# One VectorE product instead of two, moved between two scans, in a selective-scan network

## The chip, the cores and the metric

The kernel runs on one core of a Trainium2 chip. The metric is the device time of one execution in microseconds (us), less being better. The core has five engines that run their own instruction streams and meet at semaphores: TensorE (PE) multiplies matrices into PSUM, VectorE (DVE) and ScalarE (ACT) work on PSUM and SBUF, GpSimd (POOL) on SBUF, and SyncE (SP) issues the DMAs. Each stream runs in its written order: an instruction that waits holds up all behind it on its engine.

## The reference

Four images of 56 x 56 tokens with 96 channels go through two state-space blocks and two blocks of linear attention with a quantised feed-forward part. Nearly all the time is in the selective scans. Cut to that:

```
# for each of 2 layers, 4 images, 4 directions; L = 3136 tokens, 192 channels d, 16 states s
dt  = softplus(W_dt @ dt_raw + bias)            # [d, t]
h_t = exp(dt_t * A[d, s]) * h_{t-1} + dt_t * u_t * B_t[s]
y_t = sum over s of h_t[d, s] * C_t[s]           # summed over directions, plus u * D
# around it: layer norm and projection in; gate, projection, norm, GELU feed-forward out (layer 0);
# a depthwise 3x3 convolution with SiLU ahead of the scan, fusion and layer norm after it (layer 1)
```

## The kernel before, in words

**Rounds.** A scan of 3136 tokens is cut into 7 chunks of 448 tokens. A chunk is 8 rounds: two halves `e` of the channels (96 each) times four groups `q` of states. A round holds 96 channels x 4 states as three tiles of 128 partitions (`g` = 0, 1, 2) by 448 tokens. In all there are 2 x 4 x 4 x 7 x 8 = 1792 rounds.

**What a round does.** `products(n)` makes `du * B` on VectorE for g = 0 and 1, two instructions of 128x448 (L695), with B spread over the partitions in PSUM by one matmul (`spread_b`, L597, one PSUM buffer `b`). The product for g = 2 is made on GpSimd in `begin` (L690), from a copy of B in SBUF. Three scans on VectorE (L702) turn products and decays into states `h`. A decay is `exp(dt * A)` on ScalarE (`decay`, L654), into one PSUM buffer per g. After each scan of round n, ScalarE makes the same decay of round n + 1. Behind the third scan it also keeps the last column (`kept`, L672), and copies the carry into the tile of round n + 2 (`carried`, L667). GpSimd multiplies all three tiles by C in one instruction (`hc`, L744), and TensorE sums over the states (`add_up`, L775), two rounds later. Tiles `h` and `hc` have three buffers each.

**B and C.** `fetch` copies B and C from DRAM to all partitions of a tile `cb`, four DMAs per tile (L533). A tile is used in two rounds of the chunk, `q` and `q + 4`. `prepare(ch, o)` does the steps of a chunk by the number `o` of the round relative to its first: at -9 the rows of B and C go to DRAM, at -5 to -3 step sizes are parked in DRAM and spread over partitions (`dt`, `du`), and at -3 to 0 `fetch` is called. `prepare_on_scalar` and `on_tensor` do the ScalarE and TensorE steps of the same plan (L568 and L489, L590 and L479).

**Side work.** The other stages (norms, projections, GELU, convolutions, attention, feed-forward) run as generators, called lanes here. The loop hands control to them twice per round: at `yield "F"`, ahead of the round's scalar steps, and at `yield "C"`, between scans 0 and 1. Steps marked F are mostly ScalarE work, steps marked C mostly TensorE and VectorE work. A planner with declared costs (`spend`, `room`, `SPARE`, `ACT_LIMIT`, `PE_LIMIT`) limits how much enters a round. A GELU or SiLU step changes ScalarE's tables and changes them back (`exp_and_ln`, L806). `keep_busy` gives TensorE filler matmuls on zeros (L762) in rounds with little of its work. A convolution reads its rows through a window tile `win` (L930).

**Order.** The streams of TensorE, ScalarE, VectorE and GpSimd are in the order in which the code emits them. SP's order is the scheduler's. The lines that fix the order around the change:

```
            products(n)                 # top of round n
            ...                         # prepare, lane steps F, prepare_on_scalar, filler
            begin(n + 1)                # spread_b and GpSimd's product of round n + 1
            ...                         # add_up(n - 2), on_tensor
            for g in range(NG):
                if g == 1:
                    yield "C", n, r
                ...
                scan(n, g)
                ...
                decay(n + 1, g)
            carried(n + 2)
```

Of the kernel before, what the change touches and what calls it, by code (L numbers as in the profile page):

```python
# [11 lines left out]
F32 = mybir.dt.float32  # L12
# [4 lines left out]
ALU = mybir.AluOpType  # L17
# [10 lines left out]
NQ = 4  # L28
# [4 lines left out]
CS = 448  # L33
# [3 lines left out]
NCS = L // CS  # L37
RANK = (12, 6)
NW, LATE_NW = 13, 20
NWIN = 3  # L40
OWN = ()
OWN_TAIL = ()

SPARE = (0.9, 2.4)
ACT_LIMIT, PE_LIMIT = 4.0, 7.0
# [121 lines left out]
class Net:  # L167
    def __init__(self, ctx, tc, aps, at, out):
# [5 lines left out]
        self.dram = pool("dram", bufs=1, space=bass.MemoryType.DRAM)  # L174
        self.nw, self.nwin, self.depth, self.banks, self.ring = NW, NWIN, DEPTH, BANKS, None
        self.setup()
# [350 lines left out]

    def fetch(self, ch, q):

        t = self.sp.tile([128, 2, CS], F32, name="cb", bufs=5)  # L530
        rows = ch.cd.rearrange("(k n) t -> n k t", k=2)
        for s in range(4):
            self.nc.sync.dma_start(t[32 * s : 32 * s + 32], rows[q + 4 * s].partition_broadcast(32))  # L533
        ch.cb.append(t)

    def prepare(self, ch, o):

        nc = self.nc  # L540
        if o == -14:
            self.parameters(ch)
        elif o == -12:
            self.inputs(ch)
        elif o == -9:
            ch.cd = self.dram.tile([2 * NS, CS], F32, tag="cd", name="cd", bufs=3)
            nc.sync.dma_start(ch.cd, ch.cf[: 2 * NS])
        elif o == -5:
            self.times_u(ch)
            ch.dtd = self.park(ch.dtc)  # L550
        elif o == -4:
            ch.dud = self.park(ch.duc)
            self.spread_dt(ch, 0)
        elif o == -3:
            self.spread_du(ch, 0)
        elif o == 0:
            self.spread_du(ch, 1)
            self.spread_dt(ch, 1)
        if -3 <= o <= 0:
            self.fetch(ch, o + 3)  # L560

    def prepare_on_scalar(self, ch, o):

# [30 lines left out]
    def spread_b(self, ch, q):  # L594

        ps = self.psum.tile([128, 512], F32, tag="b", name="b", bufs=1)[:, :CS]
        self.nc.tensor.matmul(ps, self.sel[:, q], self.upper(ch.cf), start=True, stop=True)  # L597
        return ps
# [5 lines left out]
    def scans(self):  # L604

        nc, sp = self.nc, self.sp
        chunks = []
        for l in range(2):
            for i in range(NB):
                for n, (orient, rev) in enumerate(ORDER[l]):
                    for step in range(NCS):
                        ch = Step()
                        ch.l, ch.i, ch.orient, ch.rev, ch.step = l, i, orient, rev, step
                        ch.k = 2 * orient + rev if l == 0 else orient + 2 * rev  # L620
                        ch.c = NCS - 1 - step if rev else step
                        ch.n, ch.first = n, n == 0 and step == 0
                        ch.skip = n == 0
                        ch.last = n == 3 and step == NCS - 1
                        ch.cb, ch.dt, ch.du = [], [], []
                        chunks.append(ch)
        rounds = [(ch, e, q) for ch in chunks for e in range(NE) for q in range(NQ)]
        per = NE * NQ


        da = [self.psum.tile([128, 512], F32, name=f"da{g}")[:, : CS + 4] for g in range(NG)]
        for t in da:
            nc.vector.memset(t, 0.0)

        def steps(n):

            return [(ch, n - per * j) for j, ch in enumerate(chunks[max(0, n // per) : n // per + 3], max(0, n // per))]

        def ahead(n):
            for ch, o in steps(n):  # L640
                self.on_tensor(ch, o)

        for n in range(-14, 0):
            for ch, o in steps(n):
                self.prepare(ch, o)
            for ch, o in steps(n):
                self.prepare_on_scalar(ch, o)
            ahead(n)

        def decay(n, g):  # L650

            if n < len(rounds):
                ch, e, q = rounds[n]
                nc.scalar.activation(da[g][:, INNER], ch.dt[e][:, g], AF.Exp, scale=ch.par.na[:, e, q, g : g + 1])  # L654

        def column(t, at):

            return t[:, at : at + 2 * ROW + 1 : ROW]

        def carried(n):  # L660

            if n < len(rounds):
                ch, e, q = rounds[n]
                hs[n] = sp.tile([128, WIDE], F32, name="h", bufs=3)
                if not ch.step:
                    return
                nc.scalar.copy(column(hs[n], ROW if ch.rev else 1), ch.par.carry[:, e, q])  # L667

        def kept(n):
            ch, e, q = rounds[n]  # L670
            if ch.step < NCS - 1:
                nc.scalar.copy(ch.par.carry[:, e, q], column(hs[n], 2 if ch.rev else CS + 1))  # L672

        def own(n):
            ch, e, q = rounds[n]
            return NQ * e + q in (OWN_TAIL if ch.l and ch.i else OWN)

        hs, bs = {}, {}

        def tokens(t):  # L680

            return self.groups(t, 2)[:, :, :CS]

        def begin(n):

            if n < len(rounds):
                ch, e, q = rounds[n]
                bs[n] = self.spread_b(ch, q)
                if not own(n):
                    nc.gpsimd.tensor_tensor(tokens(hs[n])[:, 2], ch.du[e][:, 2], ch.cb[q][:, 1], ALU.mult)  # L690

        def products(n):
            ch, e, q = rounds[n]
            for g in range(3 if own(n) else 2):
                nc.vector.tensor_tensor(tokens(hs[n])[:, g], ch.du[e][:, g], bs[n], ALU.mult)  # L695

        def scan(n, g):
            ch, e, q = rounds[n]
            c = 1 if ch.step else 0
            way = slice(CS + 1 + c, 1, -1) if ch.rev else slice(2 - c, CS + 2)  # L700
            h = hs[n][:, g * ROW :]
            nc.vector.tensor_tensor_scan(h[:, way], da[g][:, way], h[:, way], 0.0, ALU.mult, ALU.add)  # L702

        carried(0)
        carried(1)
        begin(0)
        self.exp_and_ln()
        self.tables = True
        for g in range(NG):
            decay(0, g)  # L710
        late = []
        for n, (ch, e, q) in enumerate(rounds):
            r = NQ * e + q
            products(n)
            for c, o in steps(n):
                self.prepare(c, o)
            self.half_round()
            strided = [1.5 + 1.5 * ch.orient] * (r % NQ == 2)
            strided += [1.5 + 1.5 * c.orient for c, o in steps(n) for _ in self.projected(c, o)]
            self.spend((0.6, 0.7, 1.7, 0, 0, 0, 0.7, 0.6)[r], (1.3, 1.3, 0, 0, 0, 0, 0.4, 0.4)[r] + sum(strided))  # L720
            yield "F", n, r
            for c, o in steps(n):
                self.prepare_on_scalar(c, o)
            ended = late.pop(0) if len(late) == 2 else None
            if ended:
                self.keep_busy(ended[2])
            begin(n + 1)
            if ended:
                self.add_up(*ended)
            ahead(n)  # L730
            self.half_round()
# [3 lines that stand above are left out]
                if g == 2 and ended and ended[2] == NQ - 1:  # L735
                    self.spend(0.6, 0)
                    self.keep_sums(*ended[:3])
                scan(n, g)
                if g == 2:
                    kept(n)  # L740
                decay(n + 1, g)
            carried(n + 2)
            hc = sp.tile([128, NG, CS], F32, name="hc", bufs=3)
            nc.gpsimd.tensor_tensor(  # L744
                hc, tokens(hs[n]), ch.cb[q][:, 0].unsqueeze(1).to_broadcast([128, NG, CS]), ALU.mult,
            )
            late.append((ch, e, q, hc))
            del hs[n], bs[n]
        for ended in late:
            self.add_up(*ended)  # L750
        self.keep_sums(ch, e, q)
        yield "C", len(rounds), 0
# [619 lines left out]
```

## Time and profile before

| what | value |
|---|---|
| median of 3 runs | 8361.93 us (8339.22 to 8369.98) |
| the profiled execution, its own time | 8364.46 us |
| its span from first to last instruction | 8362.7 us |
| first and last scan | 112.8 and 7983.9 us |
| mean granted TensorE clock | 0.898 of full |
| one scan, mean duration (L702) | 1071 ns, 5376 of them |
| one product with B, mean duration (L695) | 604 ns, 3584 of them |
| one decay, mean duration (L654) | 632 ns, 5376 of them |
| one `hc` (L744) and one GpSimd product (L690) | 2726 and 979 ns, 1792 of each |

In rows of groups, the columns after the count are the busy time in us, the mean duration in ns of one instruction, and the idle time of the engine just before them with what ended it. Instructions overlap at their ends, so a start-to-start distance is a little shorter than a duration. In rows of waits, the columns are the total in us, the number of times, and the longest. In a timeline, a row has its start, its length, the engine, the line, what is written and read, how many instructions are merged, and in brackets the idle time ahead. About 380 us after the last scan are side work of the last image, which the change does not touch.

### The profile page before, as it was taken

Reading aid. Unit: us, or ns where it says so; the run is one execution under the profiler, and the core shown is the slowest. Engines: PE = TensorE matmul, PEld = TensorE weight load, DVE = VectorE, ACT = ScalarE, POOL = GpSimd, SP = SyncE. Lnnn points to the kernel's source line nnn. Section 1 sums busy time; section 2 is a strip of 40 time slices with the busy share of each in tenths; the row PEclk is TensorE's granted clock in tenths of the full one; section 3 lists DMA queues with packets and bytes.
Section 4 is the critical chain, followed back from the end, with each engine's and each line's share of the span. In section 5 each row is a group of like instructions: output and inputs, shape, how many; then the busy total and the mean of one; then the engine's idle time right before and its main releaser. Section 6 shows DMA issues by size and latency. Waiting matters only on the chain. (4 is left out here: it accounts for less than half of the span.)

```text
span 8362.7 us, 119228 instructions
## 1 busy us (share of the span) xinstructions
PE 7469.6 (89%) x33633; PEld 2721.6 (33%) x33633; DVE 7516.6 (90%) x9555; ACT 6109.8 (73%) x12807; POOL 7177.3 (86%) x3991
## 2 busy tenths in 40 slices
PE   7889888898889988898899979988899888998997
PEld 3333233232333223232322323333333333333344
DVE  5999999999998999999998999999999999999921
ACT  5778878776787768786777766777776777767736
POOL 4999989989998999899898998998888888889820
PEclk8899989899999989998898989988899888999986
DMA  5777777678766777677776777676766667666721
GB/s 154 179 188 189 203 179 182 167 175 199 178 174 170 172 188 181 172 177 184 177 175 167 174 185 176 166 170 172 186 166 162 166 173 182 167 160 167 175 57 48
DMA packets 944159, 1417.77 MB, mean 170 GB/s; under 512 B 169410, under 2 KB 936644, under 8 KB 942628
## 3 DMA queue, kind: packets, MB, share of 16 engines
q1 hardware_dynamic: 942720, 1408.34, 68.2%
q8 instruction: 264, 4.33, 0.2%
q14 instruction: 403, 3.30, 0.1%
q10 hardware_dynamic: 772, 1.80, 0.1%
HBM read 1141.42 MB, written 268.14 MB: 169 GB/s over the span
## 5 line engine op out<-in xcount | busy, mean ns | idle before, releaser
L702 DVE TENSOR_TENSOR_SCAN h<-da,h 128x449 f32<-128x449 f32 (+1 forms) x5376 | 5507.1, 1071 | 134.9 <-ACT da L654 79.3
L744 POOL TENSOR_TENSOR hc<-h,cb 128x1344 f32<-128x1344 f32 x1792 | 4884.8, 2726 | 598.8 <-DVE h L702 413.6
L654 ACT ACTIVATE da<-dt,na 128x448 f32<-128x448 f32 x5376 | 3353.1, 632 | 1143.2 <-DVE h L702 1104.4
L695 DVE TENSOR_TENSOR h<-du,b 128x448 f32<-128x448 f32 x3584 | 2019.6, 604 | 182.7 <-PE b L597 112.6
L775 PE MATMUL y<-hc,four 128*32 128x448 f32 x14336 | 1913.0, 609 | 17.8 <-POOL hc L744 17.4
L690 POOL TENSOR_TENSOR h<-du,cb 128x448 f32<-128x448 f32 x1792 | 1754.1, 979 | 141.4 <-DMA cb<-cd 110.1
L762 PE MATMUL y<-w,zeros 128*96 128x448 bf16 x4843 | 1354.0, 397 | 0.0
L597 PE MATMUL b<-cf,sel 128*128 128x448 bf16 x1792 | 680.2, 380 | 631.2 <-DVE h L695 626.6
L762 PEld LDWEIGHTS <-zeros 128*96 128x96 bf16 x4843 | 603.2, 135 | 1111.0 <-issue 965.1
L775 PEld LDWEIGHTS y<-hc,four 128*32 128x32 f32 x14336 | 294.2, 113 | 1182.5 <-issue 660.5
L433 PE MATMUL pp<-U,wd 96*128 96x448 f32 x896 | 664.5, 830 | 12.1 <-DMA U<-u 8.3
L771 PE MATMUL y<-Y,ident 96*96 96x448 f32 x672 | 542.9, 898 | 18.6 <-ACT Y L782 14.3
L919 PE MATMUL ps<-win,dg 64*64 64x220 f32 (+11 forms) x1998 | 547.3, 471 | 0.0
L479 PE MATMUL pp<-cf,wd 12*96 12x448 f32 (+1 forms) x896 | 476.2, 613 | 71.7 <-ACT dtc L489 47.6
L672 ACT COPY carry<-h 128x3 f32<-128x3 f32 x1536 | 301.9, 197 | 282.3 <-DVE h L702 276.2
L504 POOL TENSOR_TENSOR duc<-dtc,U 96x896 f32<-96x896 f32 x224 | 483.1, 2157 | 3.3 <-ACT dtc L491 3.3
L782 ACT COPY Y<-y 96x448 f32<-96x448 f32 x448 | 341.7, 763 | 77.7 <-PE y L775 76.8
L919 PEld LDWEIGHTS ps<-win,dg 64*64 64x64 f32 (+2 forms) x1998 | 239.7, 162 | 321.5 <-issue 289.0
L667 ACT COPY h<-carry 128x3 f32<-128x3 f32 x1536 | 280.2, 182 | 66.3 <-POOL hc L744 63.5
L489 ACT ACTIVATE dtc<-pp,wd 96x448 f32<-96x448 f32 x448 | 281.7, 629 | 31.3 <-PE pp L479 27.4
L597 PEld LDWEIGHTS <-sel 128*128 128x128 bf16 x1792 | 183.8, 103 | 336.1 <-issue 272.7
L827 PEld LDWEIGHTS ps<-avg,w 96*112 96x112 f32 (+2 forms) x1944 | 249.9, 193 | 108.1 <-issue 59.0
(427 smaller groups left out, 5933.9 us busy)
## 6 DMA issues: line engine op xcount, KB each, us to landing
cb<-cd SPq DMA_DIRECT2D x3584, 112.0 KB, 3.9
dt<-dd SPq DMA_DIRECT2D x1792, 168.0 KB, 4.3
du<-dd SPq DMA_DIRECT2D x1792, 168.0 KB, 4.1
dd<-dtc SPq DMA_DIRECT2D x224, 336.0 KB, 3.0
dd<-duc SPq DMA_DIRECT2D x224, 336.0 KB, 3.1
U<-u SPq DMA_DIRECT2D x112, 168.0 KB, 4.7
z<-w SPq DMA_DIRECT2D x56, 224.0 KB, 4.5
u<-w SPq DMA_DIRECT2D x56, 224.0 KB, 3.9
```

Source lines behind the costliest of these rows:

```text
L433: self.nc.tensor.matmul(ch.ps.rearrange("p (a b) -> p a b", b=HS), ch.par.wx[:, e], self.in_order(self.U[e], ch.orient, ch.c * CS, CS), st ...
L504: self.nc.gpsimd.tensor_tensor(in_rows(ch.duc), in_rows(ch.dtc), u[:, :, lo : lo + CS // HS], ALU.mult)
L597: self.nc.tensor.matmul(ps, self.sel[:, q], self.upper(ch.cf), start=True, stop=True)
L654: nc.scalar.activation(da[g][:, INNER], ch.dt[e][:, g], AF.Exp, scale=ch.par.na[:, e, q, g : g + 1])
L690: nc.gpsimd.tensor_tensor(tokens(hs[n])[:, 2], ch.du[e][:, 2], ch.cb[q][:, 1], ALU.mult)
L695: nc.vector.tensor_tensor(tokens(hs[n])[:, g], ch.du[e][:, g], bs[n], ALU.mult)
L702: nc.vector.tensor_tensor_scan(h[:, way], da[g][:, way], h[:, way], 0.0, ALU.mult, ALU.add)
L744: nc.gpsimd.tensor_tensor(hc, tokens(hs[n]), ch.cb[q][:, 0].unsqueeze(1).to_broadcast([128, NG, CS]), ALU.mult,)
L762: self.nc.tensor.matmul(self.y[:C], self.zeros, self.some, start=False, stop=False)
L771: nc.tensor.matmul(o, w, self.in_order(a, ch.orient, ch.c * CS, CS), start=True, stop=False)
L775: nc.tensor.matmul(self.y[32 * n : 32 * n + 32], self.four, hc[:, g], start=n == 3, stop=n == 3 or q == NQ - 1,)
L919: self.nc.tensor.matmul(o[:, a - r0 : e - r0, x0:x1], diag[:, tap], win[:, a + dy - lo : e + dy - lo, x0 + dx : x1 + dx], start=n == 0, st ...
```

## The change

The two products with B of a round become one instruction over 128 x 2 x 448, and it stands ahead of the third scan of the round before. The matmul that spreads B leaves `begin` and is emitted at the end of the round two before. `fetch` is called at -6 to -3 with seven `cb` buffers instead of five. There are four window tiles instead of three. An option to do the third product on VectorE, empty before, is taken out.

```diff
-NWIN = 3
-OWN = ()
-OWN_TAIL = ()
+NWIN = 4
 ...
-        t = self.sp.tile([128, 2, CS], F32, name="cb", bufs=5)
+        t = self.sp.tile([128, 2, CS], F32, name="cb", bufs=7)
 ...
-        if -3 <= o <= 0:
-            self.fetch(ch, o + 3)
+        if -6 <= o <= -3:
+            self.fetch(ch, o + 6)
 ...
         # begin(n)
-                bs[n] = self.spread_b(ch, q)
-                if not own(n):
-                    nc.gpsimd.tensor_tensor(tokens(hs[n])[:, 2], ch.du[e][:, 2], ch.cb[q][:, 1], ALU.mult)
+                nc.gpsimd.tensor_tensor(tokens(hs[n])[:, 2], ch.du[e][:, 2], ch.cb[q][:, 1], ALU.mult)
+
+        def spread_b(n):
+            if n < len(rounds):
+                bs[n] = self.spread_b(rounds[n][0], rounds[n][2])

         def products(n):
-            ch, e, q = rounds[n]
-            for g in range(3 if own(n) else 2):
-                nc.vector.tensor_tensor(tokens(hs[n])[:, g], ch.du[e][:, g], bs[n], ALU.mult)
+            if n < len(rounds):
+                ch, e, q = rounds[n]
+                b = bs.pop(n).unsqueeze(1).to_broadcast([128, 2, CS])
+                nc.vector.tensor_tensor(tokens(hs[n])[:, :2], ch.du[e][:, :2], b, ALU.mult)
 ...
+        spread_b(0)                     # ahead of the loop
         begin(0)
 ...
+        products(0)
+        spread_b(1)
 ...
-            products(n)                 # top of round n
 ...
+                if g == 2:
+                    products(n + 1)     # in the loop over g, ahead of scan(n, 2)
                 scan(n, g)
 ...
+            spread_b(n + 2)             # end of round n
```

More of the change, by code (lines that the diff above doesn't have):

```diff
@@ L672, in kept @@
                 nc.scalar.copy(ch.par.carry[:, e, q], column(hs[n], 2 if ch.rev else CS + 1))
-        def own(n):
-            ch, e, q = rounds[n]
-            return NQ * e + q in (OWN_TAIL if ch.l and ch.i else OWN)
         hs, bs = {}, {}
@@ L687, in begin @@
                 ch, e, q = rounds[n]
-                bs[n] = self.spread_b(ch, q)
-                if not own(n):
-                    nc.gpsimd.tensor_tensor(tokens(hs[n])[:, 2], ch.du[e][:, 2], ch.cb[q][:, 1], ALU.mult)
+                nc.gpsimd.tensor_tensor(tokens(hs[n])[:, 2], ch.du[e][:, 2], ch.cb[q][:, 1], ALU.mult)
+        def spread_b(n):
+            if n < len(rounds):
+                bs[n] = self.spread_b(rounds[n][0], rounds[n][2])
         def products(n):
-            ch, e, q = rounds[n]
-            for g in range(3 if own(n) else 2):
-                nc.vector.tensor_tensor(tokens(hs[n])[:, g], ch.du[e][:, g], bs[n], ALU.mult)
+            if n < len(rounds):
+                ch, e, q = rounds[n]
+                b = bs.pop(n).unsqueeze(1).to_broadcast([128, 2, CS])
+                nc.vector.tensor_tensor(tokens(hs[n])[:, :2], ch.du[e][:, :2], b, ALU.mult)
         def scan(n, g):
@@ L747, in scans @@
             late.append((ch, e, q, hc))
-            del hs[n], bs[n]
+            del hs[n]
+            spread_b(n + 2)
         for ended in late:
```

## The prediction

> **What bounds the kernel now.** I read the engines' shares first, then the costliest groups, then who waited for whom on VectorE, then the timeline.
>
> ```profile
> PE 7469.6 (89%) x33633; PEld 2721.6 (33%) x33633; DVE 7516.6 (90%) x9555; ACT 6109.8 (73%) x12807; POOL 7177.3 (86%) x3991
> ...
> L702 DVE TENSOR_TENSOR_SCAN h<-da,h 128x449 f32<-128x449 f32 (+1 forms) x5376 | 5507.1, 1071 | 134.9 <-ACT da L654 79.3
> ...
> L695 DVE TENSOR_TENSOR h<-du,b 128x448 f32<-128x448 f32 x3584 | 2019.6, 604 | 182.7 <-PE b L597 112.6
> ...
> L690 POOL TENSOR_TENSOR h<-du,cb 128x448 f32<-128x448 f32 x1792 | 1754.1, 979 | 141.4 <-DMA cb<-cd 110.1
> ```
>
> Four engines are busy, but 5507.1 + 2019.6 us of VectorE is the round loop itself. It runs from 112.8 to 7983.9 us: 7871 us for 1792 rounds, 4.39 each. The median distance from one round's first scan to the next is 4.01 us, the bare sum of a round's five VectorE instructions: in most rounds VectorE never waits. Its gaps in the loop sum to only about 440 us. The waits:
>
> ```profile
> DVE h L695 <- PE b L597: 112.6, 143, 4.6
> DVE w L856 <- PE ps L842: 87.8, 21, 12.3
> DVE h L702 <- ACT da L654: 79.3, 165, 2.1
> DVE h L702 <- POOL h L690: 53.2, 26, 10.1
> ```
>
> (Columns: total us, times, longest; the second reaches into the stretch after the loop.) The third decides my forecast. The timeline shows where it comes from: a round in which ScalarE changes its tables.
>
> ```profile
> 2106.98 0.63 ACT L654 ACTIVATE da<-dt,na 128x448 f32<-128x448 f32 x1
> 2107.55 0.18 ACT L667 COPY h<-carry 128x3 f32<-128x3 f32 x1
> 2107.75 1.28 ACT L1038 ACT_TABLE_LOAD   x1
> 2109.04 1.16 ACT L1038 ACTIVATE w<-ps,b 128x448 f32<-128x448 f32 x2
> 2110.22 1.28 ACT L806 ACT_TABLE_LOAD   x1
> 2111.52 1.19 ACT L654 ACTIVATE da<-dt,na 128x448 f32<-128x448 f32 x2
> ```
>
> VectorE in the same stretch:
>
> ```profile
> 2106.77 1.12 DVE L695 TENSOR_TENSOR h<-du,b 128x448 f32<-128x448 f32 x2
> 2107.81 3.05 DVE L702 TENSOR_TENSOR_SCAN h<-da,h 128x449 f32<-128x449 f32 x3
> 2110.78 1.12 DVE L695 TENSOR_TENSOR h<-du,b 128x448 f32<-128x448 f32 x2
> 2112.19 1.09 DVE L702 TENSOR_TENSOR_SCAN h<-da,h 128x449 f32<-128x449 f32 x1 [0.29 <-ACT da L654]
> ```
>
> The last scan of a round ends, ScalarE makes decay 2 (L654), copies a carry, and then does side work until 2111.52; only then comes decay 0, for which the scan at 2112.19 waits. Meanwhile VectorE runs a pair of products, three scans and another pair, about 5.07 us. The burst needs 5.36, so VectorE waits 0.29.
>
> [...] a pair starts 1.04 us before the next scan (2106.77 to 2107.81)[...] after the load at 2107.75 the next instruction starts at once[...]
>
> **The change, part by part.**
>
> *One product for two: -96 us.* [...] No trace shows a 128x2x448 product[...].
>
> *The product moved ahead of the last scan: +197 us.* It leaves the gap between a round's scan 2 and the next round's scan 0. From one scan 2 to the scan 0 two rounds on, VectorE used to have two pairs and three scans, 5.07 us; now one product and three scans, 2.97 + 0.99 = 3.96. ScalarE's order is unchanged: kept, decay 2, carry, side work, decay 0. Relative to the scans, decay 2 can start one product later, while decay 0 is due at the same scan. In the burst shown the wait becomes 5.36 - 3.96 = 1.40 instead of 0.29. Going through all rounds, ScalarE's work from decay 2 to the following decay 0 exceeds 3.15 us in 231 of them (the pairs of Silu or Gelu with two table loads, and the two-fold quantised relu at L1204 to L1206). In 168 of these the scan started within 0.25 us of its decay, in 214 within 1.05. Summing 1.05 less the slack, where positive, gives 197 us. As a cross-check, the same count at the old threshold of 4.2 us gives 75 us of waiting, and the trace has 79.3. The other two decays keep their slack: each still has three scans and a product between its release and its use.
>
> *B's matmul moved from behind the filler matmuls to the end of the round two before: -40.* It is single-buffered, so it still starts after the preceding product and has three scans until it is due. But 49 of the 143 waits, 50 us, come after three or more fillers (L762, 0.28 us each) queued ahead of it. Now it goes first. Queued behind it, when it waits for VectorE, are those fillers, add_up and the next TensorE steps; they may start a product and a scan sooner than now.
>
> *That earlier start is used up by others: +40.* TensorE's steps L590 and L479 wait for ScalarE's copies of the same round, which move one product later; B is due a scan and a product earlier relative to them, in four of eight rounds. GpSimd's hc is also nearer: it is done 2.87 us after scan 2 in the median round, and TensorE will ask for it about then. Bounds 0 and +100; I take the middle.
>
> *B and C six rounds ahead, and the fourth window: -50.* The queue shows the stop that both remove:
>
> ```profile
> 2545.82 1.73 SPq L514 DMA_DIRECT2D du<-dd  x4
> 2560.92 0.47 SPq L930 DMA_DIRECT2D win<-m  x1
> 2561.48 0.53 SPq L514 DMA_DIRECT2D dt<-dd  x1
> ```
>
> A window waits for its buffer for 13.3 us (2547.6 to 2560.9); behind it wait dt and cb; GpSimd waits 12.7 for cb and VectorE 9.6 for GpSimd. Three such stops make 30 of the 53.2 us. I take 45 of these, and 5 of the 34.4 of VectorE's waits for du, of which 15.6 belong to the very first round. Moved earlier in SP's queue are four DMAs per B/C pair; q = 3 will wait for the hc of the round just ended, but du for the same round is issued in front of it and the next in three rounds, so I cost that wait at nothing. If lanes stop the queue elsewhere, du becomes the late one.
>
> *Relief of other waits in the rounds that now stall: -50.* TensorE and GpSimd catch up while VectorE waits 197 us more. The loop's waits on lane results (ps 96, ScalarE's w 38) and the rest of the B waits (about 63) are 197 us; I let a quarter go. Bounds 0 and -150.
>
> Sum: -96 + 197 - 40 + 40 - 50 - 50 = +1 us. The profiled execution took 8364.46 us (span 8362.7), 2.5 above the median of 8361.93: forecast 8365 us.
>
> **The rivals.**
>
> *Slower: ScalarE sets the pace of burst rounds, and nothing is relieved.* The mechanism is decay 0 behind a table change; it decides from 3.15 us of work on. For it: the count reproduces today's 79.3. Without relief and without B's -40, with +40 from TensorE: -96 + 197 + 40 - 50 = +91, about 8455; with the upper TensorE bound 8515.
>
> *Faster: TensorE's earlier start is worth more than its anchors cost.* For it: TensorE waits 626.6 us for the products (B's buffer) and leaves VectorE waiting for ps, w and da. If bursts fall in rounds that other engines delay anyway, half of their cost remains: -96 + 98 - 90 - 50 = -138, about 8225. Against it: slack in the burst rounds is near zero, so nothing else delays them.
>
> *The merged product is no cheaper* (two dimensions handled as two passes): the -96 goes, and with the rest about 8460. [...]
>
> **How the numbers follow.** About 0.5%, 42 us, is what a measurement of this kernel can tell from no change. The even trade 0.40, its own range 8310 to 8425 (30 of these 40 points within 0.5%, 5 on each side); slower, with the unmerged case, 0.33; faster 0.27. So faster 0.32, same 0.30, slower 0.38. The range takes in both main rivals: 8215 to 8490.
>
> **What would show it.** In the profile after: 1792 products of about 1.05 us with a start-to-start near 0.99; scan waits on da up from 79 to about 275 us, nearly all on the first scan of a round; cb and the window's waits gone; waits for b below 113. If the da waits stay under 120 the central step is wrong and the kernel is faster; if b waits double, TensorE's anchors were underrated.

## The result, and the profile after

The changed kernel takes **8580.16 us** (median of 4 runs, 8555.56 to 8585.28), against 8353.1 for the kernel before beside it: 1.0265 times as long, 95% interval 1.0236 to 1.0294. The forecast was 8365 us, with a range up to 8490; the kernel is slower than either. TensorE's mean granted clock was 0.900 in the profiled execution and 0.898 before, so the clock does not explain the loss. Lines of code have moved a little: the scan (L702) is now L701, the decay (L654) L652, the product (L695) L694, B's matmul (L597) L595.

The engines' shares and the costliest groups of the page after:

```profile
PE 7460.7 (87%) x33633; PEld 2730.5 (32%) x33633; DVE 7414.1 (86%) x7763; ACT 6081.2 (71%) x12807; POOL 7182.9 (84%) x3991
...
L701 DVE TENSOR_TENSOR_SCAN h<-da,h 128x449 f32<-128x449 f32 (+1 forms) x5376 | 5522.1, 1071 | 270.6 <-ACT da L652 262.4
...
L694 DVE TENSOR_TENSOR h<-du,b 128x896 f32<-128x896 f32 x1792 | 1904.1, 1063 | 328.5 <-PE b L595 178.2
...
L682 POOL TENSOR_TENSOR h<-du,cb 128x448 f32<-128x448 f32 x1792 | 1757.8, 981 | 46.9 <-DMA cb<-cd 27.1
```

VectorE does 102.5 us less work and is idle longer. Some of its waits (total us, times, longest; the last two also count waits outside the loop):

```profile
DVE h L701 <- ACT da L652: 262.4, 225, 1.9
DVE h L694 <- PE b L595: 178.2, 156, 5.4
DVE w L860 <- PE ps L846: 107.3, 32, 14.5
DVE h L694 <- DMA du<-dd: 51.8, 10, 22.6
```

Sorted over the stretch from the first scan to the last, in us:

| VectorE in the loop | before | after | difference |
|---|---|---|---|
| busy | 7442.9 | 7340.4 | -102.5 |
| waits of a scan for its decay | 79.3 | 262.4 | +183.1 |
| waits of a product for B | 112.6 | 178.2 | +65.6 |
| waits for lane results of TensorE and ScalarE | 124.1 | 161.1 | +37.0 |
| waits of a scan for GpSimd's product | 53.2 | 7.0 | -46.2 |
| other waits, nearly all ahead of a product | 52.6 | 124.9 | +72.3 |
| length of the loop | 7871.0 | 8078.8 | +207.7 |

(Gaps under 0.15 us are left out of the waits.)

The other waits hide more waits for B. The profile names as the releaser what it infers from semaphores, and some products that it puts down to something else, or to nothing ("issue"), start right behind B's matmul. TensorE, then VectorE:

```profile
817.66 0.36 PE L595 MATMUL b<-cf,sel 128*128 128x448 bf16 x1
818.11 1.09 DVE L694 TENSOR_TENSOR h<-du,b 128x896 f32<-128x896 f32 x1 [0.94 <-issue]
```

In the profile after, all but one of the 156 products put down to B start 0.09 to 0.11 us after its matmul ended. So do 69 products among the other waits, with 74.1 us. Before, products put down to B start 0.04 or 0.11 us after it, and 35 of the others 0.09 to 0.11 us, with 26.8 us. Counted with these, B's waits went from 139.4 to 252.3 us, +112.9. The rest went from 25.8 to 50.8, +25.0; most of it is put down to DMAs (18.8 before, 46.2 after).

The first scan starts 9.8 us later, at 122.7 us, and the part behind the last one is 2 us shorter.

The burst that the prediction showed is the same step of the same round here. ScalarE, then VectorE:

```profile
2178.63 0.63 ACT L652 ACTIVATE da<-dt,na 128x448 f32<-128x448 f32 x1
2179.20 0.18 ACT L665 COPY h<-carry 128x3 f32<-128x3 f32 x1
2179.39 1.28 ACT L1042 ACT_TABLE_LOAD   x1
2180.69 1.16 ACT L1042 ACTIVATE w<-ps,b 128x448 f32<-128x448 f32 x2
2181.87 1.28 ACT L810 ACT_TABLE_LOAD   x1
2183.16 1.20 ACT L652 ACTIVATE da<-dt,na 128x448 f32<-128x448 f32 x2
```

```profile
2176.43 1.06 DVE L694 TENSOR_TENSOR h<-du,b 128x896 f32<-128x896 f32 x1
2177.41 3.05 DVE L701 TENSOR_TENSOR_SCAN h<-da,h 128x449 f32<-128x449 f32 x3
2180.38 1.06 DVE L694 TENSOR_TENSOR h<-du,b 128x896 f32<-128x896 f32 x1
2181.36 1.08 DVE L701 TENSOR_TENSOR_SCAN h<-da,h 128x449 f32<-128x449 f32 x1
2183.83 1.09 DVE L701 TENSOR_TENSOR_SCAN h<-da,h 128x449 f32<-128x449 f32 x1 [1.39 <-ACT da L652]
```

The merged row of three scans spans a round boundary: scan 2 of one round, then scans 0 and 1 of the next. Then come the product, scan 2, and the scan 0 that waits. From the end of the first of them VectorE has one product where it had two. The burst is as long as before, and the wait is 1.39 us instead of 0.29; 1.40 was predicted for it.

### The profile page after: what moved, and what is told of

The parts are those of the page before. It is cut to its first block, busy times and chain, and to the rows that moved or that the text cites. A ratio compares the mean times of both kernels' runs of the same rounds, so it can differ in the third digit from the quotient of the medians.

```text
span 8578.1 us, 114910 instructions
## 1 busy us (share of the span) xinstructions
PE 7460.7 (87%) x33633; PEld 2730.5 (32%) x33633; DVE 7414.1 (86%) x7763; ACT 6081.2 (71%) x12807; POOL 7182.9 (84%) x3991
## 5 line engine op out<-in xcount | busy, mean ns | idle before, releaser
L701 DVE TENSOR_TENSOR_SCAN h<-da,h 128x449 f32<-128x449 f32 (+1 forms) x5376 | 5522.1, 1071 | 270.6 <-ACT da L652 262.4
L747 POOL TENSOR_TENSOR hc<-h,cb 128x1344 f32<-128x1344 f32 x1792 | 4885.0, 2726 | 896.4 <-DVE h L701 692.1
L652 ACT ACTIVATE da<-dt,na 128x448 f32<-128x448 f32 x5376 | 3325.3, 630 | 602.2 <-DVE h L701 567.7
L694 DVE TENSOR_TENSOR h<-du,b 128x896 f32<-128x896 f32 x1792 | 1904.1, 1063 | 328.5 <-PE b L595 178.2
L766 PE MATMUL y<-w,zeros 128*96 128x448 bf16 x4843 | 1295.0, 384 | 0.0
L595 PE MATMUL b<-cf,sel 128*128 128x448 bf16 x1792 | 692.7, 387 | 436.5 <-DVE h L694 433.2
L766 PEld LDWEIGHTS <-zeros 128*96 128x96 bf16 x4843 | 638.4, 132 | 1105.2 <-issue 893.0
L477 PE MATMUL pp<-cf,wd 12*96 12x448 f32 (+1 forms) x896 | 478.4, 615 | 185.1 <-ACT dtc L487 104.4
L595 PEld LDWEIGHTS <-sel 128*128 128x128 bf16 x1792 | 191.3, 107 | 659.8 <-issue 655.8
L665 ACT COPY h<-carry 128x3 f32<-128x3 f32 x1536 | 278.4, 181 | 43.4 <-POOL hc L747 41.2
L477 PEld LDWEIGHTS pp<-cf,wd 12*96 12x96 f32 (+1 forms) x896 | 114.0, 166 | 587.4 <-ACT dtc L487 235.5
```

What stands on the lines that cost most here:

```text
L477: self.nc.tensor.matmul(ch.pd, ch.par.wt[rows, C * e : C * e + C], ch.cf[rows], start=True, stop=True)
L694: nc.vector.tensor_tensor(tokens(hs[n])[:, :2], ch.du[e][:, :2], b, ALU.mult)
L747: nc.gpsimd.tensor_tensor(hc, tokens(hs[n]), ch.cb[q][:, 0].unsqueeze(1).to_broadcast([128, NG, CS]), ALU.mult,)
L766: self.nc.tensor.matmul(self.y[:C], self.zeros, self.some, start=False, stop=False)
```

## The experiments

Theory 1: the product's new place takes a product's length of slack from ScalarE's bursts, and some from TensorE. Rivals: B's new place is the cause, the early fetch is the cause, or VectorE's shorter round merely meets the pace of the others.

### The merge alone

```diff
-            for g in range(3 if own(n) else 2):
-                nc.vector.tensor_tensor(tokens(hs[n])[:, g], ch.du[e][:, g], bs[n], ALU.mult)
+            b = bs[n].unsqueeze(1).to_broadcast([128, 2, CS])
+            nc.vector.tensor_tensor(tokens(hs[n])[:, :2], ch.du[e][:, :2], b, ALU.mult)
```

> The kernel before with the two products as one instruction of 128x2x448 at the same place (top of the round); nothing else is changed. If the merge saves what VectorE's busy time lost in the changed kernel (7516.6 to 7414.1, 102 us), this run is about 1.2% faster than before, 8250 to 8270 us. If instead the freed VectorE time only turns into waits for TensorE and ScalarE, it is within 0.4% of before. Waits for decays stay near 80 us and waits for B near 113 us in both.

Measured: 8474.61 us, 1.0136 of before (1.0121 to 1.0151). Both expectations missed: the merge alone makes the kernel slower. VectorE's timeline in this run:

```profile
2003.34 1.06 DVE L695 TENSOR_TENSOR h<-du,b 128x896 f32<-128x896 f32 x1
2004.51 3.06 DVE L702 TENSOR_TENSOR_SCAN h<-da,h 128x449 f32<-128x449 f32 x3
2007.48 1.06 DVE L695 TENSOR_TENSOR h<-du,b 128x896 f32<-128x896 f32 x1
```

From the product's start to the scan's it is 1.17 us, with a gap between them (2003.34 + 1.06 = 2004.40). In the changed kernel it is 0.98 (2176.43 to 2177.41). Over all pairs without a long wait the medians are 1.166 and 0.979 us. Behind the merged product stands the scan that reads it. With two products, that scan read the first one, which takes 0.604 us and had ended while the second ran; so the pair cost 1.04. The median round grows from 4.01 to 4.14 us. In the loop, busy time and gaps under 0.15 us together grow by 184.4 us, and shorter waits (421.8 to 351.6 us) give back 70.2. So here the merge pays only with something between the product and its reader; the run with the product two rounds ahead, below, confirms it.

### The product back, with and without B

The product goes behind the third scan. In the first run B's matmul also goes back behind the filler:

```diff
-        spread_b(1)                     # first run only, ahead of the loop
 ...
+            spread_b(n + 1)             # first run only
             begin(n + 1)
 ...
-                if g == 2:
-                    products(n + 1)
                 scan(n, g)
 ...
+            products(n + 1)
             carried(n + 2)
 ...
-            spread_b(n + 2)             # first run only
```

> The changed kernel with the merged product back behind the third scan and the spreading of B back behind the filler, so that of the change there remain the merge, the early fetch and the fourth window. Theory 1 (the product's place takes a product's length away from ScalarE's bursts): the waits for decays fall from 262 to about 80 us and the time is 1.5 to 2% below before, 8190 to 8240 us. Theory 2 (TensorE and B's place are the cause): also faster, but then the next run, which leaves B's new place, stays slow. Theory 3 (the early fetch and its queue order are the cause): it stays above 8450 us.

> The changed kernel with only the product moved back behind the third scan; the spreading of B stays at the end of the round, behind that product. Theory 1: as fast as the run with both moved back, within 0.5%, with decay waits near 80 us. Theory 2: waits for B stay near 178 us and the time stays above 8400 us, whatever the decays do.

Measured: 8444.98 us, 1.0105 of before (1.009 to 1.012), with both back; 8465.59 us, 1.0124 (1.01 to 1.0149), with the product alone. They agree within their intervals, so with the product between the rounds B's new place in TensorE's stream costs nothing that can be told from zero. Decay waits are 64.0 and 84.2 us, B waits 66.6 and 50.9. The levels expected were too low by more than 200 us, since the merged product again stands right ahead of its reader (median 1.166 us in the second of them). A median round of 4.14 us also gives everyone else time, so these low waits don't show what the place costs at 4.01.

### The old fetch and three windows in the changed kernel

```diff
-NWIN = 4
+NWIN = 3
-        t = self.sp.tile([128, 2, CS], F32, name="cb", bufs=7)
+        t = self.sp.tile([128, 2, CS], F32, name="cb", bufs=5)
-        if -6 <= o <= -3:
-            self.fetch(ch, o + 6)
+        if -3 <= o <= 0:
+            self.fetch(ch, o + 3)
```

> The changed kernel with the old fetch (three rounds ahead, five buffers) and three windows; product and B as in the change. If the early fetch and the fourth window are worth the 46 us that VectorE's waits behind GpSimd's product lost (53.2 to 7.0), this run is about 0.5% slower than the changed kernel, 8610 to 8640 us. Theory 3: it is faster than the changed kernel by over 1%, under 8490 us.

Measured: 8579.66 us, 1.0276 of before (1.0249 to 1.0303): the same as the changed kernel's 1.0265. Both expectations missed: the fetch is not the cause, and it gains nothing either. VectorE's wait for GpSimd's product is back at 36.8 us, but the loop starts at 113.4 us again and B and decay waits are 168.7 and 256.3.

### The move without the merge

```diff
-                b = bs.pop(n).unsqueeze(1).to_broadcast([128, 2, CS])
-                nc.vector.tensor_tensor(tokens(hs[n])[:, :2], ch.du[e][:, :2], b, ALU.mult)
+                b = bs.pop(n)
+                for g in range(2):
+                    nc.vector.tensor_tensor(tokens(hs[n])[:, g], ch.du[e][:, g], b, ALU.mult)
```

> The changed kernel with its one product cut into two of 128x448 again, at the new place ahead of the third scan. VectorE's bare round is then 4.01 us, as before. Theory 1 (the place itself takes slack from ScalarE and TensorE): the waits for decays stay at 200 to 260 us and those for B at 130 to 180, and the time is 3 to 3.5% above before, 8600 to 8660 us. Rival (the waits rise only because VectorE's bare round fell to 3.95 us and it now meets the pace of the others): with 4.01 us again the waits fall back to about 80 and 113 us, and the time is near or just below before, 8310 to 8370 us.

Measured: 8642.1 us, 1.034 of before (1.0322 to 1.0358). A round without waits takes 4.01 us, as before, and yet:

```profile
DVE h L702 <- ACT da L652: 250.3, 228, 1.7
DVE h L695 <- PE b L595: 172.7, 150, 6.4
```

Theory 1 holds, and the rival that blames the shorter round falls. With these runs the two halves of the change can be set beside each other (the fetch differs between cells, which the run with the old fetch shows to matter little):

| | two products | one product |
|---|---|---|
| between the rounds | before, 1 | 1.0136 (1.0121 to 1.0151) |
| ahead of the third scan | 1.034 (1.0322 to 1.0358) | 1.0265 (1.0236 to 1.0294) |

The move costs by itself. The merge costs at the old place and gains at the new one. With the early fetch in all four cells, from other runs of this document, the picture is the same: 0.9986 and 1.0105 between the rounds, 1.034 and 1.0265 ahead of the third scan.

### Without table loads

Every GELU and SiLU of the side work becomes an identity, and the loads behind them go, in the kernel before and in the changed one. Both runs thus leave out a part of the computation. In short:

```diff
-            nc.scalar.activation(g[0], ps[0], AF.Gelu, bias=self.b1[:, :1])
-            self.exp_and_ln()
+            nc.scalar.activation(g[0], ps[0], AF.Identity, bias=self.b1[:, :1])
```

> The kernel before with every GELU and SiLU of the side work replaced by an identity and the table loads behind them left out, so that part of the computation is left out. ScalarE's bursts shrink by two loads of 1.28 us. The decay waits fall from 79 to under 30 us, what remains coming from the quantised relu pairs; the time falls by 50 to 100 us, to 8260 to 8310 us.

> The changed kernel with the same functions and table loads left out. Theory 1: the decay waits fall from 262 to 60 to 100 us (the relu pairs stay), and the distance to the kernel before without tables shrinks from 220 to under 100 us: 8330 to 8400 us. Rival (VectorE's shorter round meets TensorE and GpSimd): the decay waits fall, but others take their place and the distance stays at 180 us or more, above 8450 us.

Measured: 8278.28 us for the kernel before (0.991, 0.9895 to 0.9925) and 8329.73 us for the changed one (0.9975, 0.9965 to 0.9984). The distance between the two shrinks from 227 to 51 us, and the decay waits of the changed kernel from 262 to 53:

```profile
DVE h L694 <- PE b L595: 174.3, 164, 5.4
...
DVE h L701 <- ACT da L652: 53.4, 65, 1.9
```

This takes away the suspected cost and leaves the rest in place. Three quarters of the net loss go with the table loads. B's waits hardly change with them (with the hidden ones 229.1 us, against 124.3 in the kernel before without loads), so they have another cause. Nor do the waits for lane results fall: 177.6 us, against 112.9. The profile of the changed kernel without loads is of its slowest execution, 0.4% above its median.

### TensorE's plan steps behind B

```diff
-            ahead(n)                    # behind add_up
             self.half_round()
 ...
             spread_b(n + 2)
+            ahead(n)
```

> The changed kernel with TensorE's steps of the plan (the projections, L588, L477), which wait for ScalarE's copies of the same round, moved from ahead of the side work to behind the spreading of B at the end of the round. If B is late because it stands behind these waits, VectorE's waits for B fall from 178 to under 90 us, those for lane results fall too, and the time falls by 60 to 120 us, to 8460 to 8520 us; decay waits stay near 260. If B is late because TensorE has too much work in a row (convolutions, quantised layers), B's waits and the time stay within 20 us of the changed kernel.

Measured: 8507.92 us, 1.0183 of before (1.0165 to 1.02), 72 us less than the changed kernel:

```profile
DVE h L701 <- ACT da L652: 297.7, 259, 3.6
...
DVE h L694 <- PE b L595: 60.9, 66, 4.3
DVE h L694 <- issue: 57.7, 59, 5.5
```

The waits put down to B fall by 117 us, but part of that only changes its name, as the last line shows. Counted by the end of B's matmul, as above, they fall from 252.3 to 160.6, by about 92 us. B stood behind steps that wait for ScalarE's copies. TensorE's waits show this, before and then in the changed kernel:

```profile
PE pp L479 <- ACT dtc L489: 47.6, 29, 2.9
PE pp L590 <- ACT cf L568: 25.0, 21, 2.6
PE pp L479 <- ACT cf L568: 23.1, 29, 3.6
```

```profile
PE pp L477 <- ACT dtc L487: 104.4, 111, 3.8
PE pp L588 <- ACT cf L566: 87.8, 67, 4.0
PE y L779 <- POOL hc L747: 86.8, 94, 3.3
PE pp L477 <- ACT cf L566: 79.4, 106, 4.2
```

Not all of the 92 us is gained: ScalarE now waits for the later steps (for L588 and L477, 134 and 106 us), and decay waits grow by 35.

### Slack put back: the early fetch alone, and three other orders

The kernel before with only the fetch and the window of the change:

> The kernel before with only the early fetch, seven buffers for B and C and the fourth window; products and B as before. If this part is worth what VectorE's wait behind GpSimd's product lost, about 46 us, less the some 8 us by which the loop starts later in the kernels with the early fetch: 8300 to 8330 us. If the waits for B and lane results take it up again, it stays within 20 us of before.

Measured: 8342.57 us, 0.9986 of before (0.9977 to 0.9996). A gain, but of about 11 us. The wait for GpSimd's product fell from 53.2 to 9.9 us. Against it stand more waits for B (112.6 to 126.3), for du (18.8 to 39.7 in the loop) and for decays (79.3 to 86.0), and a loop that starts 6.9 us later.

The merged product between the rounds, but made for the round after the next:

```diff
-                hs[n] = sp.tile([128, WIDE], F32, name="h", bufs=3)
+                hs[n] = sp.tile([128, WIDE], F32, name="h", bufs=4)
 ...
-                if g == 2:
-                    products(n + 1)
                 scan(n, g)
 ...
-            carried(n + 2)
+            products(n + 2)
+            carried(n + 3)
 ...
-            spread_b(n + 2)
+            spread_b(n + 3)
```

Ahead of the loop, products, carries and B are made for one round more. `cb` has five buffers and the old fetch, to make room.

> The changed kernel with the merged product between rounds again, but for the round after the next: a fourth h buffer, the carry copied three rounds ahead, B spread three rounds ahead at the end of the round. To make room B and C are fetched as before the change (five buffers, three rounds ahead); four windows stay. The scan behind the product reads another tile, so the 0.19 us between a merged product and the scan that reads it should be gone, and ScalarE keeps its two products of slack. If both costs were what they were taken for: bare round 3.95 us, decay waits 80 to 110 us, B under 130, time 8200 to 8290 us. If the place between the rounds costs in another way, above 8350 us.

Measured: **8268.76 us**, 0.9894 of before (0.9869 to 0.9919), faster than both kernels. The burst in this run:

```profile
2101.01 1.06 DVE L694 TENSOR_TENSOR h<-du,b 128x896 f32<-128x896 f32 x1
2101.98 3.05 DVE L701 TENSOR_TENSOR_SCAN h<-da,h 128x449 f32<-128x449 f32 x3
2104.95 1.06 DVE L694 TENSOR_TENSOR h<-du,b 128x896 f32<-128x896 f32 x1
2106.43 1.09 DVE L701 TENSOR_TENSOR_SCAN h<-da,h 128x449 f32<-128x449 f32 x1 [0.42 <-ACT da L652]
```

From the product to the next scan it is 0.97 us, since that scan reads the tile made a round earlier. Two products lie between the third scan of one round and the first of the round after next, and the burst's wait is 0.42 us. Decay waits are 125.9 us, a little above the 80 to 110 expected, B's 59.5 (79.1 with the hidden ones), and a round without waits takes 3.95 us, as in the changed kernel. TensorE's mean granted clock was 0.924 in this execution, against about 0.90 in those of the kernel before; how much of the gain goes with that was not separated.

The same with TensorE's plan steps behind B:

> The run with the product two rounds ahead, and TensorE's plan steps behind the spreading of B as well. If those steps hold B up here as they did in the changed kernel (72 us), a further 20 to 70 us, 8150 to 8250 us; if they do not, since B has the slack of before here, within 20 us of the run without this.

Measured: 8571.08 us, 1.0262 (1.0246 to 1.0277), a clear miss. B's waits were already low. Now ScalarE waits for the late steps, and every decay behind that wait is late; VectorE waits 340.4 us for decays. ScalarE's waits:

```profile
ACT dtc L487 <- PE pp L477: 406.8, 345, 5.4
ACT cf L566 <- PE pp L588: 362.6, 265, 8.8
```

Last, in the changed kernel, ScalarE's side work moved to where the slack now is, with the plan steps behind B:

```diff
-            yield "F", n, r             # ahead of prepare_on_scalar
 ...
-            ahead(n)
-            self.half_round()
 ...
                 if g == 2:
+                    self.half_round()
+                    yield "F", n, r
                     products(n + 1)
 ...
             spread_b(n + 2)
+            ahead(n)
```

> The changed kernel with ScalarE's side work moved from ahead of decay 0 to behind decay 1, where the product now gives slack, and TensorE's plan steps behind B. If slack in the wrong place is the cost, decay waits fall to about 100 us and the time to 8250 to 8350 us. If the side work, now right behind TensorE's side work of the same round, waits for TensorE and holds up decay 2, decay waits stay over 200 us and the time is above 8450 us.

Measured: 8572.41 us, 1.0263 (1.0245 to 1.0282). Decay waits fell to 78.7 us, as the first theory had it, but the time did not:

```profile
DVE h L694 <- ACT h L665: 344.8, 266, 5.7
DVE w L860 <- PE ps L846: 94.1, 25, 12.0
DVE h L701 <- ACT da L652: 78.7, 79, 3.6
```

The burst now stands ahead of the carry copy (L665) in ScalarE's stream. The product writes the same tile and waits for it, and it stands ahead of the scan that the delayed decay is for, so the copy is due first. Neither expectation had seen that wait.

## Why the prediction was wrong

By its own steps, all in the loop:

- **The product, -96 us: right.** It was the author's estimate, and so was the 0.99 us from a merged product to the next scan: no trace of the kernel before shows either. Busy time fell by 102.5, and the start-to-start time is 0.979 us, against 1.044 for a pair. What was not seen is that this saving depends on the place: right ahead of its reader the merged product costs 1.166 us. The rival that called the merge no cheaper looked at dimensions (one product over both takes 1063 ns, each of the two took 604), not at the reader.
- **The product's place, +197: right**, mechanism and size. The decay waits grew by 183.1 us, nearly all on the first scan of a round (260.4 of the 262.4 us), the burst shown waits 1.39, and without table loads the distance to the kernel before falls to 51 us.
- **B behind the filler, -40, and TensorE's anchors, +40: wrong, and the largest miss.** The two were to cancel, and B's waits grew by 112.9 us, of which the profile names 65.6. The anchor term was undersized: moving the steps that wait for ScalarE takes about 92 us off these waits. The prediction named the mechanism and a bound of +100, and took the middle. Its own sign for this, B's waits doubling, nearly came: they are 1.8 times those before. It also started from 112.6 us of waits for B where there were 139.4.
- **Fetch and window, -50: half right.** The wait behind GpSimd went, -46.2 us. The later start of the loop, +9.8, and the +25.0 of other waits, most of them put down to DMAs, were missing; for du the prediction had counted a gain of 5. Together that leaves -11. Alone this part is worth 11 us, and in the changed kernel nothing that can be told from zero.
- **Relief, -50: wrong in sign.** VectorE's longer waits relieved nobody: waits for lane results rose by 37.0 us, and B's with them. The rounds that stall on table loads are not what raised them: without the loads the decay waits are down to 53.4 us, and lane waits are 65 us and B's 105 us above those of the kernel before. The rise goes with the product's new place: with two products a round and the early fetch, lane waits are 123.8 us at the old place and 156.6 at the new one. Through which engine it comes stays open.

So two terms failed: B with TensorE's anchors, taken at nothing and worth +112.9, and relief, taken at -50 and measured at +37.0. The terms that were held to cancel were +1 us in the sum. With what they measured it is -102.5 + 183.1 + 112.9 + 37.0 - 46.2 + 25.0 = +209.3, and the later start makes 219 of it, less 2 behind the loop and 2 of small gaps. That is the difference of the spans, 8578.1 - 8362.7 = 215.4. The slower rival had the right mechanism, with 8455 us, and 8515 at its upper bound; what it lacked are the longer waits for lane results (+37.0), the other waits (+25.0) and the later start.

## What to carry to other kernels

Here one instruction moved in VectorE's stream moved slack in the others (waits for decays +183.1 us, for B +112.9): look for each engine's longest stretch between two points of contact, and count what the moved instruction covered there. Merging these two instructions took away the distance to the reader that the second one gave the first, so the merged one needed other work behind it (0.979 us to the next scan instead of 1.166); making it a round earlier, with one more buffer, kept both the saving and the slack. If a prediction is a sum of gains and losses that cancel, do not count stalls as relief for the others without a wait that shows it: here the other waits grew while VectorE stalled. And before a wait is called unexplained, look at what ended just ahead of it: 74.1 of the 252.3 us of waits for B stood under other names.

## What the runs showed of the hardware

A scan that reads the product just ahead of it on VectorE started 0.187 us later than one that does not read it (1.166 us from the product's start in the run with the merge alone, 0.979 in the changed kernel, medians). A product of 128x2x448 with B broadcast over the middle dimension takes 1063 ns, against 604 for 128x448, and the next scan starts 0.979 us after it, where it reads another one, against 1.044 for a pair (medians). GpSimd's product takes 981 ns beside the merged product and 979 beside the two, its `hc` 2726 in both. A table load is 1.28 us here, and the instruction behind it starts 0.012 us after its end (median of the loads, in the kernel before and in the changed one).
